# Four placements in a four-layer graph network: gate biases' loads, first variances' roots, score dots, and x + 0.5

## The chip, the cores and the metric

The kernel runs on one core of a Trainium2 chip. Its engines work side by side: TensorE (PE; its weight loads are listed apart as PEld), VectorE (DVE), ScalarE (ACT), GpSimd (POOL) and SyncE (SP). Here SP issues loads through a hardware queue (q1 in the profile) and POOL issues loads, stores and accumulating loads through a software queue (q0); both are served by the same 16 DMA engines. The metric is the device time of one execution in microseconds. All data are 32-bit floats.

## The reference

A graph of N = 2708 nodes, 512 features each, with a weighted adjacency matrix `adj` of 2708 x 2708. Four layers, each added to its input, and each fed with `relu(layernorm(x))`:

```python
h = relu(layernorm(x))
x = x + relu(D0 (adj + I) D0 h W0)          # D0 = (rowsum(adj) + 1) ** -0.5
h = relu(layernorm(x))
x = x + (D1 adj D1 h) W1.T + b1             # D1 = (rowsum(adj) + 1e-8) ** -0.5
h = relu(layernorm(x))
x = x + relu(D2 (adj + I) D2 h W2)
h = relu(layernorm(x))                      # layer 3, with the sums s = adj h
g_a = sigmoid([s, h] Wa.T + ba)             # one gate per node
g_b = sigmoid([s, h] Wb.T + bb)
e   = where(adj != 0, exp(-leaky_relu(h W_sa a_l + (h W_sa a_r).T)), 0)
x = x + sigmoid(g_a * (e / rowsum(e)) h W_sa + g_b * (adj h W_g + b_g))
```

`ba` and `bb` are single numbers; they are needed in layer 3 alone. The products with `adj` (2708 x 2708 x 512, once per layer in layers 0 to 2, twice in layer 3) are the bulk of the work.

## The kernel before

**Tiles.** The nodes are cut in four quarters of five 128-row tiles (`KT = 5`) plus a tail that fills tiles `NF` and `NF + 1`. There are 22 node tiles in all (`NT`); two tail tiles hold the rows that are left from the quarters. Each quarter of columns is worked in two pieces `u` of width `W = 339`. A block `yb[j, q, u]` of the adjacency matrix is 128 x 5 x 339 elements (847.5 KB).

**Products.** The product of a layer's `h` with the adjacency matrix is done by a scheme of seven products in place of eight, on two levels. The outer seven (`OUTER`) run over the quarters in pairs; the inner seven are in `multiply`: for one piece `u` it does, in this order, `pa` (operands 1), `pb` (6), `pa` again (2), `pc` (7), `pd` (5), `pc` again (4) and `pd` again (3). Each of these is a `product` of five accumulating matmuls of 128x128 by 128x339 (the profile lists each as two instructions, 10 in all). The operands are sums: `inner_x` makes s1 to s4 out of `h` (VectorE), `inner_y` makes t1 to t4 out of four blocks of the matrix (VectorE, four adds of 128 x 1695 per piece). `s3` alone comes from `inner_x3`. Results leave through v and u2, u3 and `agg`.

**Start.** `first_aggregate` loads the first blocks while it does the row sums. For each quarter `q` and piece `u`, `degrees` takes four blocks: rows 2 and 3 into borrowed places, and the two blocks of the pair's own quarters into `y11`, and calls `column_sums`, which sums them on TensorE with a matrix of ones (`first`, four column groups at a time) into `dg_ps` (L323) and has ScalarE copy them out (L324). At piece 0 the first statistics of `x` are taken (`first_x`, `first_stats`: means and variances in `mv0`). At piece 1 `quarter_columns` lays the sums out as columns (`across`, VectorE L330 to L334), and `first_h` turns them with tiny matmuls against ones into degrees per row (`pd`, L394, one column each), takes reciprocal roots of degree and variance (`rsqrt`: ScalarE's root at L223 and VectorE's reciprocal with a Newton step, L224 to L229), makes the scale `rstd` and the shift `sh`, and has ScalarE write the normalised `h` (L254). At (q, u) = (0, 1) the first products `pas` of both pieces run, and at (1, 0) `inner_y` makes the operands of piece 0. After both quarters `pc` of piece 0 (operand 7) is put out, held behind the last matmul of the degrees (`issue_after(at_pd[-1])`), and `multiply` runs with it; `inner_y` and `pc` of piece 1 come after the first `multiply`. Meanwhile `accumulated` loads blocks "y22" (SP) and adds "y12" to them in the load itself (POOL, accumulating DMA, L770): that is t3 of the outer scheme. `other_degrees` then does the sums of the other quarters and `add_loops` (L462) adds self loops to the diagonal.

**Order.** Each engine runs its instructions in a fixed order. The program is built in the order of its Python text, and a scheduler orders each engine's instructions by its own costs; `tc.issue_after(x)` keeps what is in its block behind instruction `x` in that order. Which place of memory is used is settled by lists (`free`, `places`, `take`).

**Between layers.** Beside the outer products of one layer run the tail ends of the layer before: `next_pair` multiplies two node tiles of `agg` with the layer's weights, again by seven products (`part`, L1029, of 128x256), with sums of the weights made in place of the weight block w12; `next_alone` does a last single tile with `tile_product` (`po`, L202 to L209) and needs w12 itself, so `again_w12` (L963) loads it once more by POOL. Then `finish` adds, takes the statistics and calls `after(t, y)`. Hooks, a table from outer product to function, run extra work at a certain outer product: `second_weights` (L1120) loads layer 1's weights, bias b1 and both gate biases into `bab`; `third_weights`, `make_vs` and `fourth_weights` prepare the later layers.

**Score dots.** The scores and the h parts of the gates of layer 3 are dots of each node tile of `h` with four vectors. `h_dots` (L1161) does for each tile four multiply-and-sum passes on VectorE (L1165), adds `bab` to the two gates' columns and halves them (L1168, L1169). `behind` tells which tiles' dots follow the end of which node tile of layer 2 (`keep_h`); other tiles are in the hooks 3 of layer 2, 1 (`fourth_weights`), 7, 2 and 4 of layer 3.

**Attention.** At the end `attention_of_pair` does two node tiles of the last weight product (`pair_product`, a generator that yields between its seven products) and ScalarE and VectorE form the result. `loads` fetches x and the other branch's sum and adds 0.5 to x on ScalarE (L1478).

Of the kernel before, what the change touches and what calls it, by code (L numbers as in the profile page):

```python
# [8 lines left out]
FP = mybir.dt.float32  # L9
# [3 lines left out]
P = 128  # L13
# [8 lines left out]
U = 2  # L22
# [15 lines left out]
def gnn_kernel(  # L38
# [106 lines left out]
    def take(places):  # L145

        places.append(places.pop(0))
        return places[-1]
# [168 lines left out]
    def column_sums(ps, tls, blocks, to):  # L317


        ops = tls + [blk[:, k, :] for blk in blocks for k in range(KT)]  # L320
        for n, y in enumerate(ops):
            g = slice(n % 4 * 32, n % 4 * 32 + 32)
            nc.tensor.matmul(ps[g], first, y, start=n < 4, stop=n >= len(ops) - 4)  # L323
        nc.scalar.copy(to, ps)  # L324
# [18 lines left out]

    y11 = {}

    def degrees(q, u, ps, tls, places):

        blocks = [take(places) for _ in range(2)]
        for k in range(2):
            nc.sync.dma_start(blocks[k], yb[2 + k, q, u])  # L350
        for j in (q, 1 - q):
            y11[j, q, u] = blk = free.pop(0)
            nc.sync.dma_start(blk, yb[j, q, u])
            blocks.append(blk)
        column_sums(ps, tls, blocks, parts[0, u])
        add_loops(y11[q, q, u], u, 1)
# [29 lines left out]

    def first_h(columns, looped):

# [16 lines left out]
        mv = mv0[:, span, :]  # L405
        rstd = rstd_of(mv, n)
        nc.vector.tensor_mul(rstd[:, :n], rstd[:, :n], dinv[:, span])
        sh = shift_of(mv, rstd, n, at_shift)

# [111 lines left out]
    def inner_y(blks, u, loops, t3=None, t3_first=False):  # L521
# [10 lines left out]
        at_y.append(nc.vector.tensor_add(t4, o21, t2).ins)  # L532
        if not t3_first:
            at_y[-1] = nc.vector.tensor_add(t3, o22, o12).ins  # L534
# [30 lines left out]
    def multiply(xs_, ys, u, dests, beside=None, begun=None):  # L565
# [28 lines left out]
        if beside is not None and beside[0] == 1:  # L594
            beside[1]()
        slot()
        pb = bank("pb")
        product(pb, xs_[6], ys[6], True)
        u2 = upool.tile([P, W], FP, tag="u2", name="u2", bufs=2)
        at_u2.append(nc.vector.tensor_add(u2, v, pb).ins)  # L600
        slot()
        product(pa, xs_[2], ys[2], False)
        give(0, 0, pa, None, None)
        slot()
# [115 lines left out]
    def first_aggregate(before_fifth, between):  # L720
# [12 lines left out]
        for q, u in pieces:  # L733
# [3 lines left out]
            if u == 0:  # L737
                first_x(ts)
                first_stats(ts)
            else:  # L740
                first_h(quarter_columns(q, [parts[0, v] for v in range(U)]), 0)
            if (q, u) == (0, 1):
# [4 lines left out]
                s3 = inner_x3(XA)  # L747
            if (q, u) == (1, 0):
                ys = inner_y([y11[a, b, u] for a, b in QUAD], u, 0, own_t3, True)
        pc = bank("pc")  # L750
        with tc.issue_after(at_pd[-1]):
            product(pc, s3, ys[7], True)
        blks = {u: [y11[a, b, u] for a, b in QUAD] for u in range(U)}
# [37 lines left out]
        xs_ = inner_x(XA, s3)  # L791
        multiply(xs_, ys, 0, [p1], begun=(pas[0], pc))
        with tc.issue_after(at_u2[-1]):
            ys = inner_y(blks[1], 1, 0, own_t3)
        came[1] = accumulated(dict(zip(QUAD, t3[1])), "y22", 1, "y12")
        pc = ps_out.tile([P, W], FP, tag="out", name="pc")
        with tc.issue_after(at_pe[-1]):
            product(pc, xs_[7], ys[7], True)
        multiply(xs_, ys, 1, [p1], begun=(pas[1], pc))
        with tc.issue_after(at_v[-1]):  # L800
# [210 lines left out]
    def next_pair(ts, ws, scale, bias, src, colscale, after):  # L1011

        xts = [load_x(t, src) for t in ts]
        (a11, a12), (a21, a22) = (
# [35 lines left out]
        pc = pair_bank("pc", n)  # L1050
        part(pc, 7, True)
        nc.vector.tensor_add(u3, u2, pc)
        yield
# [15 lines left out]
    def next_alone(t, cs, scale, bias, src, colscale, after):  # L1069

        if t == NF:
            again_w12()
        xt = load_x(t, src)
# [45 lines left out]
    def second_weights():  # L1119
        take_w(w1)  # L1120
        nc.gpsimd.dma_start(b1_bc, b1.partition_broadcast(P))
        nc.gpsimd.dma_start(bab[:, 0:1], ba.partition_broadcast(P))
        nc.gpsimd.dma_start(bab[:, 1:2], bb.partition_broadcast(P))

# [46 lines left out]

    behind = {3: (0,), 4: (1,), 6: (2,), 7: (3,), 9: (4,)}
    behind.update({13: (7,), 14: (8,), 16: (9,), 17: (10,), 19: (11,)})

# [10 lines left out]
    def third_weights():  # L1185
# [8 lines left out]
        between_layers(dinv, None, xs, None, keep_h),  # L1194
        {1: third_weights, 2: make_vs, 3: lambda: h_dots((5, 6))},
    )
# [5 lines left out]
    def fourth_weights():  # L1202
        y_places.extend(more_y)
        for k in range(2):
# [7 lines left out]
            )  # L1212
        h_dots(range(12, 14))

# [148 lines left out]

    parts = {7: range(14, 17), 2: range(17, 20)}
    hooks = {p: lambda ts=ts: h_dots(ts) for p, ts in parts.items()}
# [109 lines left out]
    def loads(t):  # L1475
        xt = load_x(t, xs)
        y = load_x(t, xbs)
        nc.scalar.activation(xt, xt, AF.Copy, bias=0.5)  # L1478
        return xt, y

# [11 lines left out]
    def attention(t):  # L1492
        xt, y = loads(t)
        f = slice(0, D)
        pE = tile_product(t, tile_cols(agg, t), [wsa_sb[:, c, f] for c in range(NC)])
        result(t, xt, y, [(f, pE)], f)

    def attention_of_pair(ts, last=False, bank=None):
# [4 lines left out]
        halves = [slice(k * (D // 2), (k + 1) * (D // 2)) for k in range(2)]  # L1503
        for po in pair_product(xs_, ws_e, bank or pair_bank, last, bank is None):
            if po is not None and last:
# [395 lines left out]
```

## Time and profile before

Three runs took 2011.9, 2012.13 and 2012.25 us; the median is 2012.13 us. The profile is of one more execution:

| what | value |
|---|---|
| median of the runs | 2012.13 us |
| profiled execution, its own time | 2014.15 us |
| profiled execution, span of the core | 2012.4 us |
| mean granted clock of TensorE | 0.994 |
| VectorE busy | 1526.7 us, 76% |
| ScalarE busy | 470.7 us, 23% |
| GpSimd busy | 210.5 us, 10% |
| moved by DMA | 378.38 MB, mean 188 GB/s |

How to read it. A group of instructions stands as line, engine, operation, tile written and tile read, shapes and count, then time; "[1.78 <-DVE across L334]" is idle time of that engine just before, and what ended it. Matmuls are pipelined, so a group's own time is longer than the distance to the next group's start. The DMA row gives the busy share of the 16 DMA engines in tenths, one digit a slice, with GB/s below it; the clock row is the clock granted to TensorE in tenths of full speed. A row of waits is the engine and line that waited, what ended the wait, the total, how often, and the longest. A product of ten matmuls takes 2.86 us from start to start in most of the execution.

### The profile page before, as it was taken

How to read it: one execution, taken by the hardware profiler on the slowest of the kernel's cores; microseconds unless marked ns; L12 is line 12 of the kernel's file. 1: busy time of each engine (PE TensorE's matmuls, PEld its weight loads, DVE VectorE, ACT ScalarE, POOL GpSimd, SP SyncE). 2: the span in 40 equal slices, each digit the busy share in tenths (PEclk: the TensorE clock that was granted, in tenths of full speed). 3: DMA queues.
4: the chain of work that ended last, by engine and by line, in shares of the span. 5: the costliest groups of instructions: out<-in, count | busy, mean ns of one | idle time of the engine just before them, and what ended most of it. 6: DMA issues, size and time to landing. Idle time of an engine off the chain costs nothing.

```text
span 2012.4 us, 21223 instructions
## 1 busy us (share of the span) xinstructions
PE 1967.9 (98%) x7556; PEld 1321.4 (66%) x7556; DVE 1526.7 (76%) x2967; ACT 470.7 (23%) x965; POOL 210.5 (10%) x368
## 2 busy tenths in 40 slices
PE   6999999999999999999999999999999999999998
PEld 2566655776666677766666776666666666666666
DVE  4678977877676888886577898986877767766756
ACT  1440001334000022310001334000015544444412
POOL 0111110111000011210000122000000101011112
PEclk9999999999999999999999999999999999999999
DMA  9998595547454445575444657554644446455543
GB/s 378 312 380 263 177 325 184 178 156 252 164 180 156 140 148 179 188 255 175 147 153 144 210 186 245 184 175 158 218 138 137 125 127 171 122 172 147 149 122 100
DMA packets 81465, 378.38 MB, mean 188 GB/s; under 512 B 11400, under 2 KB 16668, under 8 KB 80720
## 3 DMA queue, kind: packets, MB, share of 16 engines
q1 hardware_dynamic: 49056, 245.95, 35.8%
q0 software_dynamic: 32304, 131.09, 21.5%
q8 instruction: 59, 0.97, 0.2%
q14 instruction: 46, 0.38, 0.1%
HBM read 298.17 MB, written 62.16 MB: 179 GB/s over the span
## 4 chain that ended last, share of the span: by engine, by line
PE 77%; DVE 9%; issue 6%; DMA 6%; ACT 1%; POOL 1%; DVEq 0%; POOLq 0%; SPq 0%; ACTq 0%
PE pa L559 17%; PE pc L559 17%; PE pd L559 16%; PE pb L559 9%; PE pt L628 4%; DMA obuf<-in_yb_dram 3%; PE pd L1029 2%; PE pc L1029 2%; PE pa L1029 2%; PE pa L1251 1%; PE pt L633 1%; PE pc L1251 1%; PE pd L1251 1%; DVE ends L1165 1%; PE pb L1029 1%
## 5 line engine op out<-in xcount | busy, mean ns | idle before, releaser
L559 PE MATMUL pa<-obuf,h 128*128 128x339 f32 x1360 | 412.4, 449 | 2.3 <-ACT h L254 1.4
L559 PEld LDWEIGHTS pa<-obuf,h 128*128 128x128 f32 x1360 | 256.7, 190 | 131.3 <-issue 3.0
L593 ACT COPY v<-pa 128x339 f32<-128x339 f32 x56 | 24.6, 439 | 650.3 <-PE pa L559 613.8
L559 PE MATMUL pb<-t,s 128*128 128x339 f32 x560 | 171.9, 452 | 2.0 <-DVE t L531 1.3
L559 PE MATMUL pd<-t,s 128*128 128x339 f32 x560 | 170.3, 448 | 0.0
L559 PE MATMUL pc<-t,h 128*128 128x339 f32 x560 | 169.4, 448 | 0.0
L559 PE MATMUL pd<-obuf,s 128*128 128x339 f32 x550 | 166.7, 448 | 0.1
L559 PEld LDWEIGHTS pb<-t,s 128*128 128x128 f32 x560 | 106.0, 191 | 57.0 <-DVE s L472 2.8
L559 PEld LDWEIGHTS pd<-t,s 128*128 128x128 f32 x560 | 105.7, 189 | 55.1 <-issue 3.5
L559 PEld LDWEIGHTS pc<-t,h 128*128 128x128 f32 x560 | 105.9, 189 | 53.4 <-issue 0.6
L559 PEld LDWEIGHTS pd<-obuf,s 128*128 128x128 f32 x550 | 104.0, 189 | 52.6 <-DVE agg L580 0.7
L559 PE MATMUL pc<-obuf,s 128*128 128x339 f32 x450 | 136.4, 448 | 0.0
L559 PEld LDWEIGHTS pc<-obuf,s 128*128 128x128 f32 x450 | 85.2, 189 | 41.5
L531 DVE TENSOR_TENSOR t<-obuf,t 128x1695 f32<-128x1695 f32 x55 | 105.4, 1917 | 0.2
L992 POOL DMA_DIRECT2D xs<-ends x66 | 36.1, 547 | 616.9 <-DVE mv L989 608.2
L532 DVE TENSOR_TENSOR t<-obuf,t 128x1695 f32<-128x1695 f32 x52 | 99.6, 1915 | 0.1
L600 DVE TENSOR_TENSOR u<-v,pb 128x339 f32<-128x339 f32 x56 | 28.3, 506 | 88.4 <-PE pb L559 88.1
L530 DVE TENSOR_TENSOR t<-obuf 128x1695 f32<-128x1695 f32 x48 | 92.2, 1920 | 3.9 <-DMA obuf<-osumt 3.1
L559 PE MATMUL pc<-obuf,h 128*128 128x339 f32 x320 | 94.5, 448 | 0.0
L1455 ACT ACTIVATE m<-m,hd 128x339 f32<-128x339 f32 x154 | 77.3, 568 | 68.8 <-DVE obuf L1461 58.5
L534 DVE TENSOR_TENSOR obuf<-obuf 128x1695 f32<-128x1695 f32 x45 | 86.5, 1923 | 2.5 <-DMA obuf<-in_yb_dram 1.0
L1461 DVE SCALAR_TENSOR_TENSOR obuf<-obuf,m 128x1695 f32<-128x1695 f32 (+1 forms) x34 | 62.4, 1839 | 28.7 <-DMA obuf<-in_yb_dram 16.2
(372 smaller groups left out, 3147.4 us busy)
## 6 DMA issues: line engine op xcount, KB each, us to landing
obuf<-in_yb_dram SPq DMA_DIRECT2D x132, 847.5 KB, 4.5
obuf<-osumt SPq DMA_DIRECT2D x100, 847.5 KB, 4.5
osumt<-obuf POOLq DMA_DIRECT2D x22, 847.5 KB, 10.2
xs<-ends POOLq DMA_DIRECT2D x66, 256.0 KB, 3.0
ends<-xs POOLq DMA_DIRECT2D x58, 256.0 KB, 4.1
obuf<-obuf POOLq DMA_DIRECT2D x16, 847.5 KB, 6.2
obuf<-in_yt_dram SPq DMA_DIRECT2D x28, 339.0 KB, 3.5
obuf<-in_yb_dram POOLq DMA_DIRECT2D x11, 847.5 KB, 11.4
```

Source lines behind the costliest of these rows:

```text
L530: nc.vector.tensor_add(t1, o12, o11)
L531: nc.vector.tensor_add(t2, o22, t1)
L532: at_y.append(nc.vector.tensor_add(t4, o21, t2).ins)
L534: at_y[-1] = nc.vector.tensor_add(t3, o22, o12).ins
L559: last = nc.tensor.matmul(ps, x[:, k, :], y[:, k, :], start=start and k == 0, stop=k == KT - 1, skip_group_check=not start,)
L600: at_u2.append(nc.vector.tensor_add(u2, v, pb).ins)
L628: nc.tensor.matmul(ps[c], h[:, NF, c * P : (c + 1) * P], tl[:, 0, :], start=start, stop=False)
L992: nc.gpsimd.dma_start(xs[t], xt)
L1029: nc.tensor.matmul(ps, xs_[k][:, c], ws[k][:, c], start=start and c == 0, stop=c == 1, skip_group_check=not start,)
L1251: nc.tensor.matmul(ps, xs_[k][:, c], ws[k][:, c], start=start and c == 0, stop=c == 1, skip_group_check=not start,)
L1455: nc.scalar.activation(e[:, k], row, AF.Prelu, bias=hd[:, t, 1:2], alpha=0.01)
L1461: nc.vector.scalar_tensor_tensor(b, b, 0.0, e, ALU.not_equal, ALU.mult)
```

## The change

- `second_weights`: the loads of the two gate biases get an `issue_after` behind the load of b1 (before, nothing held them in the scheduler's order).
- `degrees`: the two `y11` blocks are loaded and summed ahead of the blocks of rows 2 and 3; `column_sums` keeps its last matmul in `at_sums`.
- `first_aggregate`: at piece 0 the roots of the variances and the shifts are made (`first_scales`), ahead of the degrees that they are multiplied with; y7 (the sum for operand 7) of each piece is made as soon as its blocks are there, t1 ahead of the last columns, `pc` of piece 0 right behind the last column sum, and `pc` of piece 1 behind the last matmul of the degrees; t2 and t4 of piece 0 behind the shift. `multiply` with products begun does the second part of `pa` ahead of `pb`.
- `again_w12` is called in the last pair, behind its seventh product, and no longer at the head of `next_alone`.
- `behind`, hook 3 and the hooks of layer 3: which tiles' dots are done where.
- `loads` no longer adds 0.5; `half_more` does, in pairs behind the second yield of `pair_product`.

```diff
@@ -320,7 +320,8 @@
         ops = tls + [blk[:, k, :] for blk in blocks for k in range(KT)]
         for n, y in enumerate(ops):
             g = slice(n % 4 * 32, n % 4 * 32 + 32)
-            nc.tensor.matmul(ps[g], first, y, start=n < 4, stop=n >= len(ops) - 4)
+            last = nc.tensor.matmul(ps[g], first, y, start=n < 4, stop=n >= len(ops) - 4)
+        at_sums.append(last.ins)
         nc.scalar.copy(to, ps)
 
     def quarter_columns(q, two):
@@ -342,16 +343,18 @@
         return {t: columns(t) for t in range(q * KT, (q + 1) * KT)}
 
     y11 = {}
+    at_sums = []
 
     def degrees(q, u, ps, tls, places):
 
-        blocks = [take(places) for _ in range(2)]
-        for k in range(2):
-            nc.sync.dma_start(blocks[k], yb[2 + k, q, u])
+        blocks = []
         for j in (q, 1 - q):
             y11[j, q, u] = blk = free.pop(0)
             nc.sync.dma_start(blk, yb[j, q, u])
             blocks.append(blk)
+        for k in range(2):
+            blocks.append(take(places))
+            nc.sync.dma_start(blocks[-1], yb[2 + k, q, u])
         column_sums(ps, tls, blocks, parts[0, u])
         add_loops(y11[q, q, u], u, 1)
 
@@ -384,7 +387,13 @@
         repeat(g, G)
         return g
 
-    def first_h(columns, looped):
+    def first_scales(ts):
+
+        n = len(ts)
+        rstd = rstd_of(mv0[:, ts.start : ts.stop, :], n)
+        return rstd, shift_of(mv0[:, ts.start : ts.stop, :], rstd, n)
+
+    def first_h(columns, looped, scales=None):
 
         ts = list(columns)
         n, t0 = len(ts), ts[0]
@@ -403,9 +412,12 @@
             )
         rsqrt(dinv[:, span], deg[:, span], n)
         mv = mv0[:, span, :]
-        rstd = rstd_of(mv, n)
+        rstd, sh = scales or (rstd_of(mv, n), None)
         nc.vector.tensor_mul(rstd[:, :n], rstd[:, :n], dinv[:, span])
-        sh = shift_of(mv, rstd, n, at_shift)
+        if sh is None:
+            sh = shift_of(mv, rstd, n, at_shift)
+        else:
+            at_shift.append(nc.vector.tensor_mul(sh[:, :n], sh[:, :n], dinv[:, span]).ins)
 
         fs = slice(0, D // 2), slice(D // 2, D)
         for f in fs if t0 < half else fs[::-1]:
@@ -530,7 +542,7 @@
         nc.vector.tensor_add(t1, o12, o11)
         nc.vector.tensor_add(t2, o22, t1)
         at_y.append(nc.vector.tensor_add(t4, o21, t2).ins)
-        if not t3_first:
+        if t3_first is False:
             at_y[-1] = nc.vector.tensor_add(t3, o22, o12).ins
         return {1: o11, 2: o21, 3: o22, 4: t4, 5: t1, 6: t2, 7: t3}
 
@@ -594,13 +606,17 @@
         if beside is not None and beside[0] == 1:
             beside[1]()
         slot()
+        if begun:
+            product(pa, xs_[2], ys[2], False)
+            give(0, 0, pa, None, None)
         pb = bank("pb")
         product(pb, xs_[6], ys[6], True)
         u2 = upool.tile([P, W], FP, tag="u2", name="u2", bufs=2)
         at_u2.append(nc.vector.tensor_add(u2, v, pb).ins)
         slot()
-        product(pa, xs_[2], ys[2], False)
-        give(0, 0, pa, None, None)
+        if not begun:
+            product(pa, xs_[2], ys[2], False)
+            give(0, 0, pa, None, None)
         slot()
         if pc is None:
             pc = bank("pc")
@@ -737,19 +753,38 @@
             if u == 0:
                 first_x(ts)
                 first_stats(ts)
-            else:
-                first_h(quarter_columns(q, [parts[0, v] for v in range(U)]), 0)
+                scales = first_scales(ts)
+            if q == 1:
+                y7 = own_t3 if u == 0 else tpool.tile([P, KT, W], FP, tag="t", name="t3")
+                nc.vector.tensor_add(y7, y11[1, 1, u], y11[0, 1, u])
+                if u == 0:
+                    first_y7 = y7
+            if (q, u) == (1, 1):
+                t1, t2 = (
+                    tpool.tile([P, KT, W], FP, tag="t", name=f"t{k}") for k in (1, 2)
+                )
+                o11, o12, o21, o22 = (y11[a, b, 0] for a, b in QUAD)
+                nc.vector.tensor_add(t1, o12, o11)
+                pcs = [bank("pc"), ps_out.tile([P, W], FP, tag="out", name="pc")]
+                with tc.issue_after(at_sums[-1]):
+                    product(pcs[0], s3, first_y7, True)
+            if u == 1:
+                columns = quarter_columns(q, [parts[0, v] for v in range(U)])
+                with tc.issue_after(at_pe[-1]) if q == 1 else nullcontext():
+                    first_h(columns, 0, scales)
             if (q, u) == (0, 1):
 
                 pas = [bank("pa") for _ in range(U)]
                 for v in range(U):
                     product(pas[v], XA[:, 0:KT, 0:P], y11[0, 0, v], True)
                 s3 = inner_x3(XA)
-            if (q, u) == (1, 0):
-                ys = inner_y([y11[a, b, u] for a, b in QUAD], u, 0, own_t3, True)
-        pc = bank("pc")
         with tc.issue_after(at_pd[-1]):
-            product(pc, s3, ys[7], True)
+            product(pcs[1], s3, y7, True)
+        t4 = tpool.tile([P, KT, W], FP, tag="t", name="t4")
+        with tc.issue_after(at_shift[-1]):
+            nc.vector.tensor_add(t2, o22, t1)
+            at_y.append(nc.vector.tensor_add(t4, o21, t2).ins)
+        ys = {1: o11, 2: o21, 3: o22, 4: t4, 5: t1, 6: t2, 7: first_y7}
         blks = {u: [y11[a, b, u] for a, b in QUAD] for u in range(U)}
 
         def among(places):
@@ -789,14 +824,11 @@
                 load_rows(*(tail_place(b, u)[:, s] for s in range(2)), yt[:, :, 2 + b, u])
         first_x(range(half, NT))
         xs_ = inner_x(XA, s3)
-        multiply(xs_, ys, 0, [p1], begun=(pas[0], pc))
+        multiply(xs_, ys, 0, [p1], begun=(pas[0], pcs[0]))
         with tc.issue_after(at_u2[-1]):
-            ys = inner_y(blks[1], 1, 0, own_t3)
+            ys = inner_y(blks[1], 1, 0, y7, None)
         came[1] = accumulated(dict(zip(QUAD, t3[1])), "y22", 1, "y12")
-        pc = ps_out.tile([P, W], FP, tag="out", name="pc")
-        with tc.issue_after(at_pe[-1]):
-            product(pc, xs_[7], ys[7], True)
-        multiply(xs_, ys, 1, [p1], begun=(pas[1], pc))
+        multiply(xs_, ys, 1, [p1], begun=(pas[1], pcs[1]))
         with tc.issue_after(at_v[-1]):
             other_stats(range(half, NT), False)
         by_halves(nc.vector.tensor_sub, XA, XA, XB)
@@ -1010,6 +1042,8 @@
 
     def next_pair(ts, ws, scale, bias, src, colscale, after):
 
+        last = ts[1] == NF - 1
+
         xts = [load_x(t, src) for t in ts]
         (a11, a12), (a21, a22) = (
             [full_cols(agg[:, f, t // KT // 2, :, t // KT % 2], t) for f in range(2)] for t in ts
@@ -1049,6 +1083,8 @@
         nc.vector.tensor_sub(a12, a12, s2)
         pc = pair_bank("pc", n)
         part(pc, 7, True)
+        if last:
+            again_w12()
         nc.vector.tensor_add(u3, u2, pc)
         yield
         pd = pair_bank("pd", n)
@@ -1068,8 +1104,6 @@
 
     def next_alone(t, cs, scale, bias, src, colscale, after):
 
-        if t == NF:
-            again_w12()
         xt = load_x(t, src)
         po = tile_product(t, cs, [w_now[0][:, c, :] for c in range(NC)])
         y = new_y()
@@ -1118,9 +1152,10 @@
 
     def second_weights():
         take_w(w1)
-        nc.gpsimd.dma_start(b1_bc, b1.partition_broadcast(P))
-        nc.gpsimd.dma_start(bab[:, 0:1], ba.partition_broadcast(P))
-        nc.gpsimd.dma_start(bab[:, 1:2], bb.partition_broadcast(P))
+        last = nc.gpsimd.dma_start(b1_bc, b1.partition_broadcast(P))
+        with tc.issue_after(last.ins):
+            nc.gpsimd.dma_start(bab[:, 0:1], ba.partition_broadcast(P))
+            nc.gpsimd.dma_start(bab[:, 1:2], bb.partition_broadcast(P))
 
     aggregate(False, between_layers(dis, b1_bc, xs, dinv, None), {1: second_weights})
 
@@ -1169,8 +1204,8 @@
             nc.vector.tensor_scalar(hd[:, t, 2:4], hd[:, t, 2:4], 0.5, None, ALU.mult)
 
 
-    behind = {3: (0,), 4: (1,), 6: (2,), 7: (3,), 9: (4,)}
-    behind.update({13: (7,), 14: (8,), 16: (9,), 17: (10,), 19: (11,)})
+    behind = {3: (0,), 5: (1,), 7: (2,), 9: (3,)}
+    behind.update({11: (5,), 13: (6,), 15: (7,), 17: (8,), 19: (9,)})
 
     def keep_h(t, y):
         nc.gpsimd.dma_start(hs[t], h[:, t, :])
@@ -1192,7 +1227,7 @@
     aggregate(
         True,
         between_layers(dinv, None, xs, None, keep_h),
-        {1: third_weights, 2: make_vs, 3: lambda: h_dots((5, 6))},
+        {1: third_weights, 2: make_vs, 3: lambda: h_dots((4,))},
     )
 
 
@@ -1210,7 +1245,7 @@
                 wg_sb[:, :, k, D // 2 :],
                 wab[0:D, k : k + 1].rearrange("(c p) o -> p c o", p=P),
             )
-        h_dots(range(12, 14))
+        h_dots(range(10, 12))
 
 
     def in_four(a):
@@ -1361,7 +1396,7 @@
         h_dots(range(20, NT))
         nc.gpsimd.dma_start(bg_bc, bg.partition_broadcast(P))
 
-    parts = {7: range(14, 17), 2: range(17, 20)}
+    parts = {7: range(12, 16), 2: range(16, 20)}
     hooks = {p: lambda ts=ts: h_dots(ts) for p, ts in parts.items()}
     hooks[1], hooks[4] = fourth_weights, last_dots
     hooks[5] = lambda: again(range(0, half), slice(0, D))
@@ -1474,9 +1509,10 @@
 
     def loads(t):
         xt = load_x(t, xs)
-        y = load_x(t, xbs)
+        return xt, load_x(t, xbs)
+
+    def half_more(xt):
         nc.scalar.activation(xt, xt, AF.Copy, bias=0.5)
-        return xt, y
 
     def result(t, xt, y, parts, f, queue=nc.gpsimd):
 
@@ -1491,6 +1527,7 @@
 
     def attention(t):
         xt, y = loads(t)
+        half_more(xt)
         f = slice(0, D)
         pE = tile_product(t, tile_cols(agg, t), [wsa_sb[:, c, f] for c in range(NC)])
         result(t, xt, y, [(f, pE)], f)
@@ -1501,7 +1538,10 @@
         xs_ = sums_of_pair(ts, last_places if last else e_places)
         yield
         halves = [slice(k * (D // 2), (k + 1) * (D // 2)) for k in range(2)]
-        for po in pair_product(xs_, ws_e, bank or pair_bank, last, bank is None):
+        for k, po in enumerate(pair_product(xs_, ws_e, bank or pair_bank, last, bank is None)):
+            if k == 1:
+                for xt, _ in xys:
+                    half_more(xt)
             if po is not None and last:
 
                 result(ts[1], *xys[1], list(zip(halves, po[1])), slice(0, D), nc.sync)
```

## The prediction

> **What bounds the kernel now.** First the page's busy shares, its row of 40 slices and its row of the clock that TensorE was granted:
>
> ```profile
> PE 1967.9 (98%) x7556; PEld 1321.4 (66%) x7556; DVE 1526.7 (76%) x2967; ACT 470.7 (23%) x965; POOL 210.5 (10%) x368
> ...
> PE   6999999999999999999999999999999999999998
> ...
> PEclk9999999999999999999999999999999999999999
> ```
>
> TensorE is the bound: 1967.9 of 2012.4 us, every slice 90% or more but the first. 44.5 us are idle, and most of them lie in the first 52 us. An edit gains only where TensorE waits or runs below its clock, so I looked for those places near each edit. The start first, by its DMA in 40 slices of 1.5 us over 0 to 60 us:
>
> ```profile
> DMA  0799934999999999999999999999999999999999
> GB/s 0 167 410 399 353 131 131 362 425 423 448 432 398 429 429 416 411 425 425 420 413 389 432 443 423 394 430 412 407 407 425 420 416 429 407 421 354 246 227 216
> ...
> bab<-in_ba_dram POOLq DMA_DIRECT2D x1, 0.5 KB, 6.7
> bab<-in_bb_dram POOLq DMA_DIRECT2D x1, 0.5 KB, 7.4
> ```
>
> The stream runs at about 410 GB/s except in slices 5 and 6, 7.5 to 10.5 us (131 GB/s each), the very time in which the two 0.5 KB loads of the gate biases (issued 3.68 and 4.36 us, landed 10.34 and 11.74) are in flight. Then the timeline of TensorE where the column sums end, and windows of the same place and of a later one (us, busy and count of each engine, granted clock, DMA share, GB/s):
>
> ```profile
> 48.60 1.33 PE L323 MATMUL dg_ps<-ends,first 128*32 128x339 f32 x10 [0.72 <-DMA ends<-in_yb_dram]
> 51.72 0.38 PE L394 MATMUL pd<-ones,across 128*128 128x1 f32 x2 [1.78 <-DVE across L334]
> 51.96 0.58 PE L394 MATMUL pd<-ones,ends 128*128 128x1 f32 x4
> 52.41 4.79 PE L559 MATMUL pc<-ends,s 128*128 128x339 f32 x10
> 57.03 3.02 PE L559 MATMUL pa<-obuf,h 128*128 128x339 f32 x10
> ```
>
> ```profile
> 49.00:52.00 3.00, 1.22 (x13) 0.42 (x5) 2.63 (x12) 0.44 (x1) 0.90 (x1) 1.00 1.01 416
> 52.00:57.00 5.00, 5.00 (x15) 3.28 (x16) 1.59 (x13) 2.69 (x7) 1.73 (x2) 0.66 1.06 350
> ...
> 124.00:129.00 5.00, 5.00 (x14) 3.13 (x14) 4.19 (x16) 2.30 (x6) 0.00 (x0) 0.66 1.02 417
> ```
>
> The last sums start when the last block lands; then TensorE waits 1.78 us for VectorE's columns, does the degrees (pd), and the product pc takes 4.65 us from start to start where pa takes 2.86, at a granted clock of 0.66. Last, the waits of TensorE between 1100 and 1260 us (where the score dots lie), VectorE's only wait for a transfer between 40 and 130, and the dots' own times:
>
> ```profile
> PE po L202 <- DMA ends<-in_w_dram: 1.7, 1, 1.7
> PE pa L1029 <- ACT ends L1039: 1.7, 3, 1.1
> PE pb L559 <- DVE s L472: 0.6, 1, 0.6
> ```
>
> ```profile
> DVE obuf L462 <- DMA obuf<-in_yb_dram: 2.2, 1, 2.2
> ```
>
> ```profile
> L1165 DVE CUSTOM_DVE_ANT_0 ends<-h,ends x56: 672/686/693, 1115.4 to 1256.2; 128x512 f32<-128x512 f32 x56
> L1165 DVE DVE_READ_ACCUMULATOR2_ANT hd<- x56: 79/84/89, 1116.0 to 1256.8; 128x1 f32 x56
> ```
>
> **Gate biases.** The two loads leave the place ahead of POOL's first accumulating loads and go behind the load of b1 (issued 245.91 us). What they hold up now: four adjacency blocks follow each other by 2.06 us of landing, the one across the dip by 4.03, so 2.0 us. (By the table: (410-353) + 2 x (410-131) + (410-362) = 663 GB/s short over 1.5 us, 1.0 MB, 2.4 us.) All loads of the start stream without a gap, so all land s = 2.0 us earlier; lower end 0, if the dip belongs to POOL's first transfers whatever they are, upper 2.4. At the new place POOL issues b1, ba, a row load of x, bb, then w0. Two issues of 0.56 and 0.69 us go ahead of w0, which waited until 253.44 us after the row load's 247.05, so they fit. The engines' DMA is down to 0 to 240 GB/s between 248 and 252 us. First reads: bab 1119.1 us, w0 from 306.7. Cost 0; upper end 2.0 us if the same hole opens under the block issued at 255.30 us and landed 10.31 us later, which VectorE and then TensorE do wait for.
>
> **Start order.** The loads of rows 2 and 3 of a quarter go behind its two y11 blocks (SP issues as many, the last byte is no earlier); y7 sums, t1 and the first variances' roots go ahead of the last columns; the product pc of piece 0 is put between the last sums and pd, pc of piece 1 right behind pd. So TensorE's 1.78 us wait is filled by work it had to do anyway. Step by step, with s = 2.0: last sums end 49.93 - 2.0 = 47.9; pc 2.86, to 50.8; ten matmuls of pd at 0.112 each, to 51.9; second pc 2.86, to 54.8; pa needs h, which now follows pd by 2.03 us (VectorE's chain 52.58 to ScalarE's 54.61; the hoisted roots take few links off it) and the first normalised tiles by 0.5, so 54.5: no wait. pa to 57.6. pb needs s2 (L472), and VectorE now does t2 and t4 (1.83 us each, which it did at 46 to 50 before) between sh at 54.1 and s2: 54.1 + 3.7 + 0.74 = 58.5. So pb at 58.5, with 0.9 us idle, against 59.89, and the second pc (2.86, at 72.05 before) is done: 59.9 - 58.5 + 2.86 = 4.3 us ahead. Of that 1.8 is the clock of pc; if the second pc, now behind pd, is the slow one, 2.5.
>
> That lead meets a limit. The fourth accumulated block of t3 lands at 109.62 us, VectorE adds its diagonal by 110.25 (its wait of 2.2 us above), and TensorE's sums reach that block at 111.51: slack 1.26. The landing moves with the stream only, so the lead that passes is at most s + 1.26 = **3.3 us**. The next join, degrees at 121.44, has its columns 1.3 us early and moves with both. Behind it TensorE has no wait until past 205 us, and the lead stays. With s = 0 it is 1.3; with s = 2.4 and the warm clock 3.7.
>
> The Trainium skill ("TensorE: Matmul & The Clock Gate", the table of states in Part 1) lets the clock fall after an idle window of about 3.4 us. The rows show it at 0.66 after only 2.2 us without full matmuls, and at 124 us directly behind pd's one-column matmuls, with no wait. By the page the second pc would be warm; by the row it may be slow. The limit above makes this 0.8 us at most (2.5 against 3.3).
>
> **Score dots.** A tile is 4 x (0.686 + 0.084) + 0.3 = 3.4 us of VectorE. Nine tiles stay behind odd tiles' ends, one (4) moves to hook 3; hooks 7 and 2 of the next product get four each for three, so two tiles, 6.8 us, leave the stretch up to 1230 us. There ScalarE's copy (L1039) waits 4.6 us in two places for a buffer that dots still write, and TensorE waits for that copy, 1.7 us in all: those go. The 0.6 for s2 goes or stays; I take it gone. Against it: TensorE waits 1.7 us for the reload of w12, which is bound to the last pair's part 7 and then takes 6.98 us. The instruction order now leaves 3.7 us of TensorE's work between the two where 6.6 lay, so that wait may grow by up to 2.9; I take 1.5, half, since the stretch ahead also starts earlier. Sum -1.7 - 0.6 + 1.5 = **-0.8**, from -3 (no growth, small gaps of 0.2 to 0.5 us gone too) to +2 (full growth, and 1.4 us from the tiles moved: t2 is ready at 1285.6 us and read at 1287.56, slack 2.0 against 3.4 us more of dots).
>
> **again_w12 and x + 0.5.** The reload of w12 is named earlier, but keeps its place in POOL's order in all three layers and still waits for part 7: 0. In the last pair of attention ScalarE copies v before, not after, its two x + 0.5 (1.15 us), while VectorE waits for pb until 2001.9 anyway: 0, at worst 1.15 if the final x came to need them.
>
> **Sum.** -3.3 - 0.8 = -4.1. The profiled execution took 2014.15 us, so 2010.05 by its own time; it lies 2.0 above the median of the runs, 2012.13, for which the same difference gives **2008.0**.
>
> **Rivals.**
> - The hole in the stream moves to the next software transfer (POOL's accumulating loads at about 12 us and later): s = 0. For it: those loads are that queue's next. Against it: the hole is filled by the biases' packets alone. Start -1.3, sum -2.1: **2010.0**.
> - All waits near the dots go and the stream gains 2.4: -3.7 - 3.0: **2005.4**. For it: eight tiles now sit farther apart. Against it: the w12 reload.
> - Slower: VectorE saturates under hooks 7 and 2. It is busy 55 of 55 us between 1250 and 1305 already; if its lag there is paid in full, the two tiles become a TensorE wait of 6.8 us and one cold product (+1.8): 8.6 - 3.3 = +5.3, **2017.4**. It decides from a lag above t2's slack of 2.0 us in the first of the two products. Against it: t2 is put ahead of most of the added dots.
> - The engines' order hardly matters at these places: **2012**.
>
> **Chances.** Forecast 0.42, hole moves 0.20, all goes 0.20, slower 0.13, nothing 0.05. A measurement of this kernel tells about 0.2% from no change, 4.0 us. The forecast stands on that bound, so 0.24 of its 0.42 is faster; with 0.20 and 0.03 from the second and first rival, 0.47 faster; 0.39 within; 0.14 slower. Range: 2003.5, below which only more than every stall named could go, to 2013; the forecast's own is 2005.5 to 2010.5.
>
> **What would show it.** Right: no slice under 300 GB/s between 7 and 10.5 us, the last sums ending near 47.9, pc behind them, L462's wait for a block near 1.3 us or less and that block at about 107.6; few waits for L1039, the po wait at 2 to 4 us. Wrong: a hole elsewhere before 60 us, a second pc of 4.65 us followed by a wait above 1.3 for s2, TensorE waits for t or s between 1260 and 1350, or a gain at a place that I costed at nothing.

## The result, and the profile after

| kernel | runs | median us | ratio to before, 95% interval |
|---|---|---|---|
| before, beside it | 8 | 2012.02 | |
| changed | 8 | 2018.59 | 1.0035 [1.0024, 1.0046] |
| changed, once more, on another occasion | 12 | 2017.91 (before: 2013.68) | 1.0020 [1.0011, 1.0029] |

The change makes the kernel 4 to 7 us slower, where 4 us faster was forecast. The profiled execution took 2018.32 us (span 2016.2). Two executions of 3450 and 5319 us, of two kernels below, are in none of the medians and ratios.

Line numbers move: a product is L571 now (L559 before), a part of a pair L1063 (L1029), the dots L1200 (L1165), the copy v L605, t2 L543, s2 L484, the diagonal L474 (L462). First the start of the changed kernel, DMA in slices of 1.5 us over 0 to 60 us:

```profile
DMA  0899999999999999999999999999999999999899
GB/s 0 235 402 379 259 285 429 420 411 455 410 407 411 416 429 411 416 411 411 427 411 411 436 431 385 414 425 425 420 411 411 420 420 418 393 385 252 195 249 231
```

The hole of 131 GB/s at 7.5 to 10.5 us is gone but for a dip: 259 GB/s just ahead of its place and 285 in its first slice. TensorE's timeline behind the last sums:

```profile
47.06 1.33 PE L323 MATMUL dg_ps<-agg,first 128*32 128x339 f32 x10 [0.79 <-DMA agg<-in_yb_dram]
48.32 3.12 PE L571 MATMUL pc<-ends,s 128*128 128x339 f32 x10
...
52.31 3.10 PE L571 MATMUL pc<-t,s 128*128 128x339 f32 x10
55.25 3.02 PE L571 MATMUL pa<-obuf,h 128*128 128x339 f32 x10
58.90 3.12 PE L571 MATMUL pb<-t,s 128*128 128x339 f32 x10 [0.63 <-DVE s L484]
```

Both products pc now stand ahead of pa, both at the full clock (2.96 and 2.94 us from start to start). VectorE's longest wait for a transfer between 40 and 130 us, at the block that the forecast named as its limit, has grown from 2.2 us:

```profile
DVE obuf L474 <- DMA obuf<-in_yb_dram: 4.6, 1, 4.6
```

So TensorE's side of the start does what it should. The loss shows in TensorE's waits between 1100 and 1345 us, where three rows stood before (1.7, 1.7 and 0.6 us):

```profile
PE po L202 <- DMA ends<-in_w_dram: 2.6, 1, 2.6
PE pa L571 <- ACT v L605: 2.0, 2, 1.5
PE pb L571 <- DVE t L543: 1.6, 2, 1.2
PE pd L571 <- DVE s L587: 0.8, 1, 0.8
PE pd L1063 <- DVE ends L1076: 0.5, 1, 0.5
PE pa L1063 <- ACT ends L1073: 0.3, 1, 0.3
```

The wait for L1039's copy (L1073 now) shrank from 1.7 to 0.3 us as forecast, and five others grew or are new. The largest of them in TensorE's timeline:

```profile
1222.68 0.73 PE L571 MATMUL pc<-obuf,s 128*128 128x339 f32 x2
1226.01 2.56 PE L202 MATMUL po<-ends 128*128 128x512 f32 x4 [2.60 <-DMA ends<-in_w_dram]
1228.36 1.91 PE L1063 MATMUL pc<-obuf,agg 128*128 128x256 f32 x4
...
1243.56 3.02 PE L571 MATMUL pa<-obuf,h 128*128 128x339 f32 x10
1248.08 3.12 PE L571 MATMUL pa<-obuf,h 128*128 128x339 f32 x10 [1.50 <-ACT v L605]
1252.43 3.12 PE L571 MATMUL pb<-t,s 128*128 128x339 f32 x10 [1.23 <-DVE t L543]
```

and windows behind the first one (PE, PEld, DVE, ACT, POOL busy, granted clock, DMA share, GB/s):

```profile
1222.00:1227.00 5.00, 2.40 (x9) 1.30 (x9) 4.46 (x19) 1.99 (x3) 1.47 (x3) 1.00 0.79 278
1227.00:1231.00 4.00, 4.00 (x9) 2.31 (x8) 0.63 (x3) 0.24 (x1) 0.70 (x2) 0.57 0.75 270
```

A wait of 2.6 us for w12, and behind it 4 us at a clock of 0.57: pc L1063 takes 1.70 us from start to start for the 0.86 that four such matmuls take elsewhere. At 1248 the second part of pa now stands directly behind the first and waits until ScalarE has copied the first out (v); at 1252 pb waits for t2. VectorE's timeline shows why t2 is late:

```profile
1245.26 0.82 DVE L484 SCALAR_TENSOR_TENSOR s<-h,s 128x640 f32<-128x640 f32 x1
...
1249.04 0.82 DVE L530 TENSOR_TENSOR s<-h,s 128x640 f32<-128x640 f32 x1
...
1250.45 1.92 DVE L543 TENSOR_TENSOR t<-obuf,t 128x1695 f32<-128x1695 f32 x1
```

Before, t2 (L531) was begun at 1237.89 us, ahead of s2, s1 and s4; now it comes behind them and nine passes of the dots (1238.40 to 1249.84 us).

Over stages, taken at the instruction that stands at the same place in TensorE's order, this is what each profiled execution gained (-) or lost against the profiled execution of the kernel before, in us:

| kernel | to 130 | 130-300 | 300-1100 | 1100-1345 | 1345-end |
|---|---|---|---|---|---|
| changed | -3.1 | -0.4 | +0.9 | **+5.7** | +0.8 |
| changed, again | -5.0 | -0.8 | +0.4 | **+4.6** | +3.3 |
| dots alone | +1.6 | -2.8 | +1.6 | **+7.9** | -0.1 |
| changed, dots put back | -5.3 | -2.7 | -0.3 | **-1.1** | -0.5 |
| the same, again | -4.5 | -2.0 | +1.5 | **+2.4** | +1.2 |

Columns with no edit in them differ by up to 3 us between executions, so a single profile places a loss and the runs size it.

### The profile page after: what moved, and what is told of

Its sections match the earlier page's. It is cut to its first block, busy times and chain, and to the rows that moved or that the text cites. A ratio compares the mean times of both kernels' runs of the same rounds, so it can differ in the third digit from the quotient of the medians.

```text
span 2016.2 us, 21229 instructions
## 1 busy us (share of the span) xinstructions
PE 1969.9 (98%) x7556; PEld 1322.7 (66%) x7556; DVE 1527.4 (76%) x2969; ACT 470.5 (23%) x965; POOL 209.9 (10%) x368
## 4 chain that ended last, share of the span: by engine, by line
PE 79%; DVE 8%; DMA 7%; issue 4%; ACT 2%; POOL 1%; DVEq 0%; POOLq 0%; SPq 0%; ACTq 0%
PE pa L571 17%; PE pc L571 17%; PE pd L571 17%; PE pb L571 9%; DMA obuf<-in_yb_dram 4%; PE pt L644 4%; PE pc L1063 2%; PE pd L1063 2%; PE pa L1063 2%; PE pt L649 1%; PE pa L1286 1%; PE pc L1286 1%; PE pd L1286 1%; ACT m L1490 1%; PE pb L1063 1%
## 5 line engine op out<-in xcount | busy, mean ns | idle before, releaser
L571 PE MATMUL pa<-obuf,h 128*128 128x339 f32 x1360 | 412.8, 449 | 4.3 <-ACT v L605 2.6
L571 PEld LDWEIGHTS pa<-obuf,h 128*128 128x128 f32 x1360 | 256.6, 190 | 133.7 <-ACT v L605 4.2
L605 ACT COPY v<-pa 128x339 f32<-128x339 f32 x56 | 24.6, 439 | 660.6 <-PE pa L571 637.6
L571 PE MATMUL pb<-t,s 128*128 128x339 f32 x560 | 172.3, 453 | 3.5 <-DVE t L543 2.9
L571 PE MATMUL pd<-t,s 128*128 128x339 f32 x560 | 169.7, 448 | 0.0
L571 PE MATMUL pc<-t,h 128*128 128x339 f32 x560 | 169.6, 448 | 0.0
L571 PE MATMUL pd<-obuf,s 128*128 128x339 f32 x550 | 167.0, 448 | 0.8 <-DVE s L587 0.8
L571 PEld LDWEIGHTS pb<-t,s 128*128 128x128 f32 x560 | 106.0, 191 | 58.7 <-DVE t L543 5.7
L571 PEld LDWEIGHTS pd<-t,s 128*128 128x128 f32 x560 | 105.6, 189 | 55.4 <-issue 3.5
L571 PEld LDWEIGHTS pc<-t,h 128*128 128x128 f32 x560 | 105.9, 189 | 53.7 <-issue 0.6
L571 PEld LDWEIGHTS pd<-obuf,s 128*128 128x128 f32 x550 | 104.1, 190 | 53.5 <-DVE s L587 1.8
L571 PE MATMUL pc<-obuf,s 128*128 128x339 f32 x450 | 136.4, 448 | 0.0
L571 PEld LDWEIGHTS pc<-obuf,s 128*128 128x128 f32 x450 | 85.2, 189 | 41.3
L543 DVE TENSOR_TENSOR t<-obuf,t 128x1695 f32<-128x1695 f32 x54 | 103.4, 1915 | 0.2
L571 PE MATMUL pc<-obuf,h 128*128 128x339 f32 x320 | 94.5, 448 | 0.0
```

What stands on the lines that cost most here:

```text
L543: nc.vector.tensor_add(t2, o22, t1)
L571: last = nc.tensor.matmul(ps, x[:, k, :], y[:, k, :], start=start and k == 0, stop=k == KT - 1, skip_group_check=not start,)
```

## The experiments

Ratios are to the kernel before on the same chip, of 6 to 12 runs each against 27 to 32.

**The four parts.** The changed kernel with the old dots (`olddots`, "dots put back" in the text); the kernel before with one edit each (`dots`, `bab`, `start`):

```diff
 (dots)   -behind = {3: (0,), 4: (1,), 6: (2,), 7: (3,), 9: (4,)} ...
 (dots)   +behind = {3: (0,), 5: (1,), 7: (2,), 9: (3,)} ...   # and the hooks
 (bab)    +with tc.issue_after(last.ins):  # ba, bb behind b1
 (start)  +first_scales, pcs, order of degrees' loads ...
```

> The changed kernel with the score dots put back where they were before (everything else changed). My theory: TensorE was 3.3 us ahead at the column sums (108.6 against 111.8 us) as forecast, and lost all of it and more between 1100 and 1335 us, where the dots were moved; so without the dots' edit the kernel is 3 to 4 us faster than before, about 2008.5 us. The rival, that the start's new order costs time somewhere later (DMA traffic, clock), says 2014 us or more here. In the trace TensorE should reach 1250 us about 3 us earlier than before.

2009.95 us, **0.9987** [0.9976, 0.9997]. About 3 us faster than before: what is left of the change gains, and the loss is in the dots. Its profile is of a very fast execution (2004.64 us), where TensorE reached the place of 1250 us 9.4 us earlier than before, for the 3 expected; in a second execution it was 2.6 us.

> The kernel before with the score dots' edit alone. My theory: all of the loss is here, so it is 6 to 10 us slower than before, 2018 to 2022 us, lost in TensorE's wait for the reload of w12, in a cold clock behind it, and in waits for t, s and v near 1246 and 1330 us. The rival, that the loss needs the earlier start as well (the two halves of the program meet at another phase), says within 3 us of before.

2020.19 us, **1.0039** [1.0026, 1.0052]. The dots alone cost 7 to 8 us, with much the same waits as in the changed kernel (2.6 us for w12, 2.0 for v, 2.0 for t, 2.2 for s); no other part is needed.

> The kernel before with the gate biases' edit alone; the instruction order of every other engine is the same. My theory: the hole at 7.5 to 10.5 us closes, the blocks land 2 us earlier and TensorE gains 2 us at the column sums, so 2010 us. The rival, that the hole belongs to the first software transfer whatever it is, says no gain: 2012 us, with a hole at POOL's first accumulating load.

2011.35 us, 0.9991 [0.9982, 1.0]. In its profile the hole is closed and the last sums start 1.9 us earlier (46.71 for 48.60), but the degrees do not:

```profile
GB/s 0 185 415 380 322 334 407 416 439 446 405 425 416 402 420 425 416 407 425 422 398 407 452 428 403 432 399 402 425 425 420 398 425 425 425 336 199 246 235 211
```

```profile
46.71 1.33 PE L323 MATMUL dg_ps<-ends,first 128*32 128x339 f32 x10 [0.73 <-DMA ends<-in_yb_dram]
51.80 0.38 PE L394 MATMUL pd<-ones,across 128*128 128x1 f32 x2 [3.76 <-DVE across L334]
```

TensorE waits 3.76 us for VectorE's columns where it waited 1.78; pd starts at 51.80 for 51.72. My expectation of 2 us at the column sums is met, and they are lost 4 us later; the run's 1.6 us are not told from none.

> The kernel before with the start's new order alone (loads, first roots, y7 and t sums, the two products pc), biases, dots and x + 0.5 as before. My theory: the lead at the first pb is about 2.3 us, and 1.3 of it passes the accumulated block at 110 us: 2010.8 us. The rival, that the lead is kept whole, says 2009.7 or less; that it is all lost, 2012.

2010.8 us, 0.9987 [0.9978, 0.9996]. The time is the one expected, but by luck: the kernel before took 2012.98 us on this chip, so the gain is 2.2 us, nearer to the rival that the lead is kept whole (2.4) than to my 1.3, and the interval holds both. In its profile the lead is 2.5 us at 80 us and 1.3 us at the sums near 111 us, the size forecast for s = 0. At 130 us it is 2.6 again, because the first product behind the degrees took 2.94 us there and 4.62 before.

**Which of the dots' moves?** Two kernels, each with one half of them:

```diff
 (odd)    +behind = {3: (0,), 5: (1,), 7: (2,), 9: (3,)}, {11: (6,), 13: (7,), 15: (8,), 17: (9,), 19: (10,)}
 (odd)     hook 3: (4, 5); hooks 1, 7, 2, 4: 11-12, 13-15, 16-18, 19-21
 (later)   behind's places as before, {13: (5,), 14: (6,), 16: (7,), 17: (8,), 19: (9,)}
 (later)  +hook 3: none; hooks 1, 7, 2, 4: 10-11, 12-15, 16-19, 20-21
```

> The kernel before with the dots behind the odd tiles only as in the change (one tile per pair, none at 4, 6, 14, 16), but hook 3 with two tiles, hooks 7 and 2 with three as before; the tile left over goes to hook 4 (19 to 21). Theory A, that the loss sits in the stretch of the pairs, where the dots behind odd tiles lead to another order of TensorE's instructions: nearly the whole loss is here, 2017 to 2020 us, with a wait of about 2.6 us for w12, a granted clock near 0.6 behind it, and waits for v and t near 1250 us. Theory B, that the two tiles more under hooks 7 and 2 saturate VectorE: 2011 to 2014 us.

2018.86 us, 1.0028 [1.0016, 1.0039]: theory A's time, with its waits (2.9 us for w12, clock 0.57 behind it, 1.5 for v, 2.7 for t, and 1.7 for s).

> The kernel before with its own places behind the tiles, but hook 3 without dots and hooks 7 and 2 with four tiles each as in the change. Theory A: within 2 us of before, 2010.5 to 2014.5 us. Theory B: nearly the whole loss is here, 2017 to 2020 us, with waits for t or s after 1260 us.

2018.95 us, 1.0029 [1.0018, 1.004]: theory B's time, but only in part its place. Its profile lost 3.1 us between 1100 and 1345 us, 1.6 of them after 1260 (between 1315 and 1331, with one wait of 0.5 us for v and none for t or s). The largest losses at one place stand ahead of hooks 7 and 2, at 1197 (1.2 us) and here, where po waits for ScalarE's copy of the tail tile and four microseconds at 0.57 follow:

```profile
1238.35 1.20 PE L209 MATMUL po<-ends,all_again 128*128 128x512 f32 x2 [2.04 <-ACT ends L207]
```

```profile
1239.00:1243.00 4.00, 4.00 (x9) 2.28 (x8) 3.26 (x10) 2.85 (x7) 1.60 (x3) 0.57 0.15 54
```

So neither theory is right as stated. Either half changes the fixed order of TensorE and VectorE between 1130 and 1260 us, each in its own way, and each order meets an operand that is late; the two losses do not add (5.4 and 5.5 us alone, 7.2 together, by the medians).

**The two largest waits.** w12 won back on VectorE, in place of the load (in all three layers):

```diff
-nc.gpsimd.dma_start(w12, ...)
+nc.vector.tensor_sub(w12, w22, w12)   # w22 - (w22 - w12)
```

> The changed kernel, but w12 is won back on VectorE (w22 minus the difference that stands in its place, one subtraction of 128x512) and not loaded again; TensorE's order is the same. If the wait for w12 and the cold clock behind it cost what the profile shows (2.8 and 1.7 us at 1226 us), it is about 4 us faster than the changed kernel: 2014 to 2015 us. If the wait only moves to the next operand (VectorE is late there: u, s, t), 2017 to 2018.5.

2015.36 us, 1.0009 [1.0, 1.0018]: 2 to 5 us faster than the changed kernel (1.0020 and 1.0035). Its profile does not show where they were won. The wait for w12 is gone, but pd now waits 2.2 us for s where it waited 0.8, and the stage from 1100 to 1345 us still lost 5.1 us.

> The same subtraction in place of the reload of w12, in the changed kernel with the dots put back. The wait for w12 there was 0.5 to 1.7 us with little cold clock, so 1 to 2 us faster than with the dots put back alone: 2008 to 2009 us. If VectorE's place in line is too late for it, no gain: 2010.

2010.7 us, 0.9987 [0.9978, 0.9996]: no gain on the dots put back (0.9987), though the wait for w12 is gone from its profile.

Next, the two tiles of dots under hook 1 moved to hook 4 (`hook4`), and this together with the subtraction in all layers (`hook4_w12sub`):

```diff
 (hook4)  fourth_weights: -h_dots(range(10, 12))
 (hook4)  last_dots:      -h_dots(range(20, NT))
 (hook4)  last_dots:      +h_dots((10, 11, 20, 21))
```

> The changed kernel itself once more, on the same chip as the two beside it: 2018 to 2019 us, a ratio of about 1.003 to the kernel before.

> The changed kernel, but the two tiles of dots in hook 1 of layer 3 (10 and 11) are done at hook 4 instead, some 80 us later. TensorE's order differs from the changed kernel's only in that the second part of pa stands behind pb again in two products. If VectorE's dots ahead of t2 and s4 make the waits at 1246 to 1252 us (1.66 for v, 1.39 for t), these two go and the one at 1329 (0.69): 3 to 3.7 us faster than the changed kernel, 2014.5 to 2015.5 us. If the wait for w12 and the clock behind it are the whole loss, no change: 2018 us.

> The changed kernel with both: dots of hook 1 moved to hook 4, and w12 won back on VectorE. If the two waits are separate and make up the loss, the gains add: 6 to 8 us faster than the changed kernel, 2010 to 2012 us, about the time with the dots put back. If the dots behind odd tiles cost something else besides (the waits near 1130 and 1160 us), 2012.5 to 2014 us.

On the same chip: changed again 2017.91 us, 1.0020 [1.0011, 1.0029]; hook4 2014.91 us, **1.0006** [0.9998, 1.0015]; hook4_w12sub 2015.03 us, 1.0005 [0.9996, 1.0013]. Moving the two tiles gives 3 us back, as expected of the two waits at 1246 to 1252 us. They are gone from its trace (0.3 us for t is left), and TensorE's order differs from the changed kernel's only at 1248 to 1255 and 1330 to 1334 us. The stage from 1100 to 1345 us shows 0.6 to 1.7 us of the 3 (+4.0, against +5.7 and +4.6), since pd waits 1.3 us for s instead. With the subtraction as well there was no more, a miss. That stage did get shorter (+1.0), but 300 to 1100 and the end were longer than in `hook4` by 0.4 and 1.7 us.

The next kernel, `hook4_sub2`, has hook4's edit and does the subtraction in layer 2 alone; layers 0 and 1 load w12 again.

> The changed kernel with the dots of hook 1 moved to hook 4 and w12 won back on VectorE in layer 2 alone (layers 0 and 1 load it again as before). If the gain of the subtraction was eaten by the same subtraction in layers 0 and 1, where it replaces a reload that nobody waited for (0.4 to 0.9 us each in the traces), this is 1 to 2 us faster than with all three: 2012.5 to 2014 us. If the gain near 1226 us is given back after 1470 us, where these executions lost 1 to 4 us, it is 2015 us again.

2012.25 us, **0.9991** [0.9982, 1.0001], 6 us below the changed kernel's 1.0020, as if the gains add. The interval overlaps that of `hook4_w12sub`, so it is not shown that the subtraction in layers 0 and 1 made the difference. Its waits between 1100 and 1345 us:

```profile
PE pd L571 <- DVE s L587: 1.2, 1, 1.2
PE pc L1067 <- DVE ends L1092: 0.8, 1, 0.8
PE pa L1067 <- ACT ends L1077: 0.6, 1, 0.6
PE pd L1067 <- DVE ends L1080: 0.5, 1, 0.5
PE pb L571 <- DVE t L543: 0.3, 1, 0.3
```

3.4 us in all and no cold clock; the stage is 1.2 us shorter than in the kernel before. The execution lost 3.7 us after 1345 us: at 1884 us TensorE waited 2.7 us for a copy v where it waited 1.5 before, and the clock behind it was 0.57. The changed kernel, again, did much the same at 1888 us (3.0 us), which is most of its +3.3.

> The changed kernel with the dots put back, once more, beside the others on the same chip: a ratio of 0.998 to 0.9995, 2009.5 to 2012.5 us. The difference to hook4_sub2 is what the dots behind odd tiles and the fuller hooks 7 and 2 still cost: 1 to 3 us.

> The dots put back, and w12 won back on VectorE in layer 2 alone. TensorE waited 0.5 to 1.7 us for w12 there: 0.5 to 1.5 us faster than with the dots put back alone, 2009 to 2011.5 us. If it is the same, the wait only moves to the next operand.

2010.11 us, **0.9981** [0.9972, 0.999], and 2011.09 us, 0.9988 [0.9978, 0.9997]. The dots put back has the lowest ratio of the study, 3 to 4 us faster than before; the intervals of `start` and `hook4_sub2` overlap with its own. That the subtraction adds anything to it is not shown.

## Why the forecast was wrong

- **Gate biases: right, a little large.** The hole belonged to the two loads: without them the last sums start 1.9 us earlier in `bab` and 1.5 in the changed kernel (47.06 for 48.60), for s = 2.0. The rival that it moves to the next software transfer is refuted; the sign "no slice under 300 GB/s" failed by the 285. That the edit alone would be worth little was not said in the forecast: VectorE was late too, so its gain needs the start's new order.
- **Start order: right in size, in part by luck.** Forecast and measured: first pc 47.9 and 48.32, second pc 51.9 and 52.31, pa 54.8 and 55.25, pb 58.5 and 58.90, idle ahead of it 0.9 and 0.63, the lead at 80 us 4.3 and 3.74, the lead at the sums 3.3 and 3.24 us (TensorE at 108.58 where it was at 111.81). The limit is there, but its two terms were each off and cancel: the block landed at 108.29, 1.33 us earlier and not 2.0, and the slack was 1.9 us and not 1.26. In `start` VectorE got the block 0.8 us later than before (110.47 for 109.64) and 1.3 us of lead passed all the same. The sign "L462's wait near 1.3 us or less" was wrong even so: VectorE came 3.7 us earlier and the block only 1.3, so the wait of 2.2 became 4.6. One thing was not forecast: the product behind the degrees, near 121 us, took 2.94 us in five of the ten traces with the new start (`start`, both of the dots put back, changed again, `hook4`) and 4.3 us or more in the other five and in all five with the old one. That is some 1.7 us that no term of the forecast holds, and what decides it is not shown.
- **again_w12 and x + 0.5: not contradicted.** They were not run alone. From 1900 us to the end the profiles of the changed kernel and the one before differ by 0.01 us. Near 1888 us the two x + 0.5 still stand ahead of the copy v, as before.
- **Score dots: this step failed.** "Sum -1.7 - 0.6 + 1.5 = -0.8, from -3 to +2" is +7 to +8 in the runs. Three things in it. The waits for L1039 went nearly as said. The wait for w12 grew as bounded (1.7 to 2.6 us), but I costed it as time alone: what follows such a wait can run at a granted clock near 0.6, 1.8 us more here (the matmuls of the six us behind it, against their usual distances). The largest error was "t2 is ready at 1285.6 us and read at 1287.56, slack 2.0": I took the slack from the order before and looked at one later product only. With the change t2 of the product at 1252 us had moved behind s4 and nine passes of the dots, and pa's second part ahead of pb, both to be seen in the instruction order; the price was two waits of 1.2 and 1.5 us there, one of 0.8 at 1160 and one of 0.5 at 1329. Put together, the rows of the changed kernel make up the stage's 5.7 us: w12 +0.9 and the clock behind it +1.8, v +2.0, t +1.6, s +0.8, the pair's pd +0.5, against -1.4 for the copy and -0.6 for s2, 5.6 in all. The clock is not needed for a loss: in the changed kernel, again, it stayed at 1.00 behind the wait for w12, and the stage lost 4.6 us, 4.2 of them in its rows of waits. `hook4` shows that the dots of hook 1 set the order near 1250 us: with them away the order comes back, and 3 of the 4 us.
- **The slower rival named the right engine and the wrong place.** VectorE being late was a cause, beside the load of w12, but under hook 1 and among the pairs; after 1260 us, where the rival stood, 1.0 us was lost in the changed kernel's profile and 1.7 in its second.
- **Readings beside the sum.** Of the 44.5 idle us 17.8 lie in the first 52 us, which is not most; the last slice of TensorE is under 90% too; and "2.2 us without full matmuls" is 2.5 by the rows (49.93 to 52.41). No term rests on them.

What stays open: why `later` is as slow as it is by the runs (5.5 us) when its profile, of the second fastest of nine executions, shows 2.0; where the subtraction wins in `w12sub`; how much the dots behind odd tiles still cost (hook4_sub2 and the dots put back differ by 2 us, with intervals that overlap); and why the scheduler's costs favour these orders.

## What to carry to other kernels

Where the bound engine has little wait left, do not take moving off-path work as neutral: cost it in the order that it makes, by each operand's new place, not by the slack in the old order. A wait on TensorE can have two prices, its length and the clock behind it, and the second can be nearly as large as the first (2.0 and 1.8 us in `later`). A gain that ends at a join must be followed to the next late party: in the profiles, at 80 us, the gate biases' edit alone gains nothing, the start's order 2.5 us, both together 3.7 (the times of the runs do not tell these three apart).

## What the runs showed of the hardware

- **The clock behind a wait.** Granted clock in the 4 us after one wait near 1220 to 1240 us, by its length: 1.73 us, 1.00 (before); 2.0, 0.57 (later); 2.1, 0.61 (dots put back, again); 2.6, 0.57 (changed; hook4) and 0.62 (dots alone); 2.9, 0.57 (odd). One of 2.7 us kept 1.00:

```profile
1223.00:1227.00 4.00, 4.00 (x13) 2.40 (x14) 1.60 (x5) 0.71 (x1) 1.61 (x3) 1.00 0.89 323
```

  That is the changed kernel, again. At these lengths the length does not decide. Near 1085 us each of 15 traces (kernel before, changed kernel and 13 runs) has one wait of 2.1 to 2.5 us; in seven of them the matmuls behind it slowed down, in eight they did not. The same program is among both, the changed kernel and the changed kernel, again (granted clock 0.62 and 1.00 in the 4 us that follow):

```profile
1084.19 2.07 PE L1063 MATMUL pc<-ends,agg 128*128 128x256 f32 x4 [2.15 <-DVE agg L694]
```

```profile
1082.81 1.13 PE L1063 MATMUL pc<-ends,agg 128*128 128x256 f32 x4 [2.29 <-DVE agg L694]
```

  The Trainium skill ("TensorE: Matmul & The Clock Gate", the table of states in Part 1) puts the fall after an idle window of about 3.4 us; here waits of 2.0 to 2.9 us were enough in some executions, and the measurement decides.
- **One kernel, two prices.** The dots put back waited 0.5 us for w12 in one execution and 2.1 us in the other; the second lost the clock too, and the stage from 1100 to 1345 us differs by 3.5 us.
- **Two loads of 0.5 KB** that write one number into each of 128 partitions took about 2 us out of the stream of 16 DMA engines that the start was waiting for (131 for 410 GB/s over 3 us; 1.9 us back in `bab`).
